# A queue planner with fillers for TensorE and coupled durations, and the softmax quotient moved from GpSimd to VectorE

## The chip, the cores and the metric

The kernel runs on one core of one Trainium2 chip. The metric is the device time in microseconds of one execution, lower is better. Three runs of the kernel before took 5684.96, 5691.24 and 5709.57 us; their median is 5691.24 us.

## The reference

Input is a batch of 32 images, 56 x 56 pixels, 96 channels, all float32. Four layers follow each other:

```python
# layer 0, conditional: four experts, mixed per image
rw = sigmoid(mean(x, (1, 2)) @ Wr + br)
h = relu(bn1(x @ (rw mixes Wpw) + rw @ bpw))          # 96 -> 384
h = relu(bn2(depthwise3x3(h, rw mixes Wdw) + ...))    # 384 channels, nine taps
x = bn3(h @ (rw mixes Wpwl) + rw @ bpwl) + x          # 384 -> 96
# layer 1: x + depthwise5x5(x, fixed kernel)
# layer 2: relu, depthwise3x3, 96 x 96 product, batch norm
# layer 3: shifted-window attention, 7 x 7 windows, 3 heads of 32, then an MLP
s = softmax(q @ k.T / sqrt(32) + mask)
x = x + (s @ v) @ wo + bo                             # q, k, v from layernorm(x)
x = x + gelu(layernorm(x) @ w1 + b1) @ w2 + b2        # 96 -> 384 -> 96
```

## The kernel before

**Tiling and stages.** Each image goes through four stages, written as Python generators.

`stage_router` (line 664) loads the image as `xT` (96 x 3136), sums it on ScalarE, computes the four expert weights and mixes the weights `wmix` and `wmix2` on VectorE.

`stage_conditional` (723) works on twelve blocks, four strips of 14 image rows by three groups of 128 channels. `expand` (728) fills a padded block `h1` by TensorE and ScalarE; then come nine taps into `h2`: the first by ScalarE, the other eight by VectorE `scalar_tensor_tensor` on 128 x 784 elements, the group `h<-h,mix,h` of the profile, 96 per image. `project` (757) brings seven rows back to 96 channels, ScalarE scales them into `y`, and GpSimd adds them to `xT`.

`stage_depthwise` (831) lays four image rows and eight channels on the partitions by DMA and does both fixed convolutions with banded 32 x 32 matmuls on sixteen sub-arrays of TensorE, the group `cv<-x,band`. Its product with `pw` leaves eight row blocks `res`, each of seven image rows in four packs of 98 tokens.

`stage_swin` (979) does, for each of the eight blocks, layernorm (`normalized`, 929, with the power -0.5 on GpSimd), transposes, `wq`, `wk`, `wv`, scores, exponentials on ScalarE, and `kept` (1061), the mask as a product on GpSimd. `averaged` (1076) forms the denominators `pd` (96 x 392, by a matmul with ones) and the unnormalised averages `po` in two PSUM banks. `divided` (1109) makes the quotient, `attended` (1167) multiplies by `wo` and adds to `res` on VectorE (`res<-mm,res`). `hidden` (1178) and `perceptron` (1198) are the MLP; its sum is `tb<-mm,tb`, which goes out by DMA.

**The quotient.** The reciprocal of `pd` is ScalarE's exp(-ln(pd)), improved by one Newton step, out = (-po) r (pd r - 2). ScalarE takes ln and exp, copies `pd` to `den` and `-po` to `num` in SBUF, both with the pixels reordered from windows to rows. GpSimd multiplies `den` by r and `num` by r (the group `hid<-hid,hid`), and VectorE does the last `scalar_tensor_tensor`, `oT<-hid,hid`. The division of block i - 2 is recorded in round i of the loop (line 1311), the averages of block i - 1 after it (1319).

**What sets the order.** Nothing is issued while the stages run. `Recorder.call` (286) notes each instruction with its engine, its buffers, a planned duration from `cost` and `COST` (144) and a target. `interleave` (1352) runs the stages of four images beside each other and sets the target to image number + start + length x progress, by `PLAN` (155). `order` (333) is a list scheduler: each engine that is free takes the instruction with the lowest target whose producers are done, `CROSSING` (156) or `TO_TENSOR` (157) ns earlier, and whose buffers are free. The result is the fixed order of each engine's queue. `give` (421) issues it, so nearly every record in the profile has line 427 and is told apart by its tiles. Rings of buffers limit the run ahead: five PSUM banks `mm` and three `cv` (448), five `hid` (455), two `oT` (465).

A test on the weights selects a general version of layer 3 at run time; with these inputs it doesn't run.

Of the kernel before, what the change touches and what calls it, by code (L numbers as in the profile page):

```python
# [105 lines left out]
def tile_scores_in_range(ctx: ExitStack, tc: tile.TileContext, a: dict, flag: bass.AP):  # L106
# [35 lines left out]


COST = {
    ("vector", "scalar_tensor_tensor"): (180, 1.28), ("vector", "tensor_tensor"): (180, 0.96),
    ("vector", "tensor_scalar"): (190, 0.78), ("vector", "tensor_reduce"): (180, 0.95),
    ("vector", "tensor_copy"): (180, 1.1), ("vector", "reciprocal"): (180, 6.2),
    ("scalar", "activation"): (200, 0.72), ("scalar", "copy"): (200, 0.72),
    ("gpsimd", "tensor_tensor"): (350, 2.4), ("gpsimd", "memset"): (150, 0),
    ("sync", "dma_start"): (550, 0),  # L150
}
LANDING = 3000
IMAGE_LANDING = 12000

PLAN = {"router": (0, 1), "conditional": (0.7, 1), "depthwise": (1.8, 1), "swin": (3.6, 1)}
CROSSING = 350
TO_TENSOR = 700


def cost(engine, method, args, kw):  # L160
    if method == "preload_act_table_set":
        return 1300
    out = kw["out"] if "out" in kw else args[0]
    n = math.prod(out.shape[1:])
    if engine == "tensor":
        if method == "transpose":
            return 127
        k, m = args[1].shape[0], math.prod(args[1].shape[1:])
        if k == 32 and m == 32:
            return 68 * n / 392  # L170
        if k == 32:
            return 86
        if m == 32:
            return 75 if n < 128 else 255
        return 195 if n < 128 else 80 + 1.6 * n
    if len(args) > 3 and args[3] == ALU.pow:
        return 300 + 280 * n
    fixed, each = COST[engine, method]
    if engine == "scalar":
        if kw.get("accum_out") is not None:  # L180
            fixed += 190
        if hasattr(kw.get("scale"), "shape"):
            each += 0.37
        elif hasattr(kw.get("bias"), "shape"):
            each += 0.25
    return fixed + each * n
# [69 lines left out]
class Recorder:  # L256
# [4 lines left out]
    def __init__(self, nc):  # L261
        self.nc = nc
        self.work = []
        self.target = 0.0
        self.open = None
        for engine in self.ENGINES:
            setattr(self, engine, self.Engine(self, engine))

# [64 lines left out]
    def order(self):  # L333

        for n, w in enumerate(self.work):
            w.n = n
            w.waits = len(w.before)
            w.ready = 0.0
            for v in w.before:
                v.after.append(w)  # L340

            w.needs = list(w.starts)
            w.left = None
        for w in self.work:
            for b in w.starts:
                if b.ring.banks:
                    for u in b.users:
                        w.needs.extend(c for c in u.writes if c not in w.needs)
        for w in self.work:
            for b in w.uses:  # L350
                b.left = len(b.users)
        queues = {e: [] for e in self.ENGINES}
        free = dict.fromkeys(self.ENGINES, 0.0)
        events = []
        result = []

        def put(w):
            heapq.heappush(queues[w.engine], (w.target, w.n))

        def available(w):  # L360
            need = {}
            for b in w.needs:
                if b.slot is None:
                    need.setdefault(b.ring, []).append(b.number)
            return all(
                len(n) <= len(ring.free) and (ring.banks or max(n) < ring.begun + len(n)) for ring, n in need.items()
            )

        for w in self.work:
            if not w.waits:  # L370
                put(w)
        now = 0.0
        count = 0
        while len(result) < len(self.work):
            for e in self.ENGINES:
                if free[e] > now:
                    continue
                held = []
                while queues[e]:
                    item = heapq.heappop(queues[e])  # L380
                    w = self.work[item[1]]
                    if not available(w):
                        held.append(item)
                        continue
                    for b in w.needs:
                        if b.slot is None:
                            b.ring.free.sort()
                            b.slot = b.ring.free.pop(0)[1]
                            b.ring.begun += 1
                    result.append(w)  # L390
                    w.start = now
                    free[e] = now + w.ns
                    heapq.heappush(events, (free[e], count, None))
                    heapq.heappush(events, (free[e] + w.landing, count + 1, w))
                    count += 2
                    break
                for item in held:
                    heapq.heappush(queues[e], item)
            assert events, "no work can start"
            now = events[0][0]  # L400
            while events and events[0][0] <= now:
                _, _, w = heapq.heappop(events)
                if w is None:
                    continue
                if isinstance(w, tuple):
                    put(w[0])
                    continue
                for b in w.uses:
                    b.left -= 1
                    if not b.left:  # L410
                        b.ring.free.append((now, b.slot))
                for v in w.after:
                    v.waits -= 1
                    lag = 0 if v.engine == w.engine else TO_TENSOR if v.engine == "tensor" else CROSSING
                    v.ready = max(v.ready, now + lag)
                    if not v.waits:
                        heapq.heappush(events, (v.ready, count, (v,)))
                        count += 1
        return result

    def give(self, tc):
# [9 lines left out]
def kernel(  # L431
# [187 lines left out]
    nc.sync.dma_start(out=wo[:C, :C], in_=a["L3_conv_wo"])  # L619
    nc.sync.dma_start(out=wo[C:, :C], in_=a["L3_conv_bo"].rearrange("(o c) -> o c", o=1))  # L620
    centre_outputs(wo)
    w1 = load([C, M], a["L3_conv_w1"], "w1")
    w2 = load([P, NB, C], a["L3_conv_w2"].rearrange("(k p) f -> p k f", p=P), "w2")
    b2 = wide("L3_conv_b2", True)
# [354 lines left out]
    def stage_swin(b, res):  # L979
# [96 lines left out]
        def averaged(i):  # L1076

            v = rows_of.pop(i)[2]
            e = exps_of.pop(i).part(*every)
            pd = chip.new(mm)  # L1080
            with chip.together():
                for h in range(NH):
                    chip.tensor.matmul(
                        pd[h * HD : (h + 1) * HD, :RT],
                        ones32[:PS],
                        e[:PS, h].rearrange("k j q -> k (j q)"),
                        start=True,
                        stop=True,
                    )
            po = chip.new(mm)  # L1090
            with chip.together():
                for j in range(NP):
                    for h in range(NH):
                        hs = slice(h * HD, (h + 1) * HD)
                        chip.tensor.matmul(
                            po[hs, j * PK : (j + 1) * PK], v[:PS, j, hs], e[:PS, h, j], start=True, stop=True
                        )

            inv, den, num = (chip.new(hids)[:C] for _ in range(3))
            sums, log = by_windows(pd[:C, :RT]), windows_by_rows(inv)  # L1100
            chip.scalar.activation(log, sums, AF.Ln, reads=(tables,))
            chip.scalar.activation(inv, inv, AF.Exp, scale=-1.0, reads=(tables,))
            chip.scalar.copy(windows_by_rows(den), sums)
            chip.scalar.activation(windows_by_rows(num), by_windows(po[:C, :RT]), AF.Copy, scale=-1.0)
            chip.gpsimd.tensor_tensor(den, den, inv, ALU.mult)
            chip.gpsimd.tensor_tensor(num, num, inv, ALU.mult)
            averages[i] = den, num

        def divided(i):
            den, num = averages.pop(i)  # L1110
            oT = turned_out[i] = chip.new(oTs)
            chip.vector.scalar_tensor_tensor(oT[:C], den, 2.0, num, ALU.subtract, ALU.mult)

        def scores(i):

# [184 lines left out]
        for i in range(NROW + 2) if not general else ():  # L1300
# [6 lines left out]
                yield 2  # L1307
            if here:
                kept(i)
            if i > 1:  # L1310
                divided(i - 2)
            if i + 3 < NROW:
                norm1(i + 3)
                yield 1
# [2 lines left out]
                yield 1  # L1317
            if 0 < i <= NROW:
                averaged(i - 1)
                yield 2.5  # L1320
            if i > 1:
                attended(i - 2)
                yield 1.5
# [41 lines left out]
    def when(stage, b):  # L1365

        start, length = PLAN[stage]
        return b + start, length


    residuals = {}
    for step in range(B + 3):
# [59 lines left out]
```

## Time and profile before

| what | value |
|---|---|
| median of 3 runs | 5691.24 us |
| profiled execution, its own time | 5690.76 us |
| its span, first to last instruction | 5689.0 us |
| mean granted TensorE clock | 0.932 |
| TensorE busy, 58442 matmul records | 5303.7 us |
| VectorE busy, 5047 instructions | 4671.9 us |
| ScalarE busy, 8033 instructions | 4098.9 us |
| GpSimd busy, 2942 instructions | 3344.3 us |
| DMA | 166.35 MB, mean 29 GB/s |

PE is TensorE's matmuls, PEld its weight loads, DVE VectorE, ACT ScalarE, POOL GpSimd, SPq the queue of SyncE, which issues the DMAs. A group is named by the tile written, an arrow, and the tiles read. A row of a group gives the count, the total busy time in us, the mean ns of one, then the engine's idle time just ahead of it and who ended most of that. One matmul of the code in float32 stands as two records. A wait row reads: who waited, for whom, us in all, how often, the longest. The clock is a share of full speed.

### The profile page before, as it was taken

The page shows a single profiled execution, that of the slowest core. Times are in us where ns is not written, and L with a number is a line of the kernel's source. Part 1 is how long each engine was busy: PE and PEld are TensorE (multiplying, and loading weights), DVE is VectorE, ACT ScalarE, POOL GpSimd, SP SyncE. Part 2 cuts the span into 40 slices and gives each one's busy share as a digit, 9 for nine tenths or more (in the row PEclk, how much of TensorE's full clock was granted, in tenths as well). Part 3 has the DMA queues.
Part 4 walks back from the last instruction along what each step waited for, and adds up shares of the span by engine and source line. Part 5 has one row for each costly group of instructions (what it writes and reads, how often), then busy time and mean ns, then how long its engine had stood idle before and what let it go on. Part 6 is the DMA issues. An engine that isn't in the chain of part 4 may idle for free.

```text
span 5689.0 us, 139721 instructions
## 1 busy us (share of the span) xinstructions
PE 5303.7 (93%) x58442; PEld 3191.4 (56%) x58442; DVE 4671.9 (82%) x5047; ACT 4098.9 (72%) x8033; POOL 3344.3 (59%) x2942
## 2 busy tenths in 40 slices
PE   3579999999999999999999999999999999999998
PEld 1245555555555555555555556555555555556566
DVE  7998788888888888888888888888889888888621
ACT  3457777777777777777777776777777777777766
POOL 2126665666665666655666665666555666665665
PEclk8789899999999999999999998999999999999999
DMA  1020111111111111111111111101111101111100
GB/s 39 20 41 20 28 32 35 32 26 24 30 33 35 31 24 25 31 32 35 31 24 25 30 33 34 33 20 28 32 33 34 33 20 28 31 33 25 25 19 23
DMA packets 482066, 166.35 MB, mean 29 GB/s; under 512 B 477439, under 2 KB 478100, under 8 KB 478356
## 3 DMA queue, kind: packets, MB, share of 16 engines
q1 hardware_dynamic: 481428, 157.32, 13.0%
q8 instruction: 464, 7.60, 0.6%
q14 instruction: 174, 1.43, 0.1%
HBM read 41.60 MB, written 38.54 MB: 14 GB/s over the span
## 4 chain that ended last, share of the span: by engine, by line
PE 39%; DVE 39%; ACT 9%; POOL 8%; issue 5%; DMA 0%; SPq 0%; DVEq 0%; POOLq 0%; ACTq 0%
DVE h L427 34%; PE mm L427 33%; PE cv L427 7%; ACT h L427 4%; POOL exps L427 4%; ACT hid L427 2%; DVE oT L427 1%; POOL hid L427 1%; DVE res L427 1%; DVE tb L427 1%; DVE var L427 1%; ACT xT L427 1%; ACT lnsq L427 1%; POOL var L427 1%; POOL xT L427 1%
## 5 line engine op out<-in xcount | busy, mean ns | idle before, releaser
L427 DVE SCALAR_TENSOR_TENSOR h<-h,mix,h 128x784 f32<-128x784 f32 x3072 | 3815.4, 1245 | 255.2 <-ACT h L427 176.9
L427 POOL TENSOR_TENSOR hid<-hid,hid 96x392 f32<-96x392 f32 x512 | 744.6, 1470 | 333.1 <-ACT hid L427 327.1
L427 PE MATMUL cv<-x,band 32*32 32x392 f32 x24576 | 916.0, 509 | 5.9 <-ACT x L427 3.7
L427 POOL TENSOR_TENSOR var<-var,mhalf 98x4 f32<-98x4 f32 x512 | 613.5, 1202 | 357.7 <-DVE var L427 181.8
L427 PE MATMUL mm<-xT,wmix 96*128 96x448 f32 (+1 forms) x1536 | 692.4, 553 | 15.7 <-ACT h L427 12.6
L427 PE MATMUL mm<-h,wmix 128*96 128x392 f32 x1536 | 608.3, 538 | 97.4 <-ACT h L427 97.4
L427 POOL TENSOR_TENSOR lnd<-res,var 98x384 f32<-98x384 f32 x512 | 518.6, 1013 | 301.3 <-PE mm L427 262.6
L427 ACT ACTIVATE hid<-mm,c 128x392 f32<-128x392 f32 x768 | 442.0, 583 | 346.4 <-PE mm L427 335.9
L427 PE MATMUL mm<-hT,w 96*128 96x392 f32 x1536 | 626.1, 511 | 27.1 <-DVE tb L427 27.1
L427 ACT ACTIVATE h<-h,biasd,s 128x784 f32<-128x784 f32 x384 | 397.5, 1035 | 350.4 <-DVE h L427 350.3
L427 POOL TENSOR_TENSOR xT<-y,xT 96x392 f32<-96x392 f32 x256 | 342.4, 1338 | 506.0 <-ACT y L427 466.1
L427 PEld LDWEIGHTS mm<-w,hid 128*98 128x98 f32 x6144 | 561.7, 167 | 57.6 <-issue 30.6
L427 ACT ACTIVATE h<-mm,bias,s 128x448 f32<-128x448 f32 (+1 forms) x768 | 538.8, 709 | 63.6 <-PE mm L427 56.7
L427 PE MATMUL mm<-w,hid 128*98 128x96 f32 x6144 | 577.3, 250 | 0.4 <-ACT hid L427 0.4
L427 ACT ACTIVATE exps<-mm 49x196 f32<-49x196 f32 x1536 | 507.1, 330 | 88.7 <-PE mm L427 64.9
L427 POOL TENSOR_TENSOR tb<-res 98x384 f32<-98x384 f32 x256 | 318.3, 1243 | 369.3 <-DMA out<-tb 193.3
L427 PEld LDWEIGHTS cv<-x,band 32*32 32x32 f32 x24576 | 331.4, 103 | 362.4 <-issue 260.0
L427 DVE TENSOR_REDUCE var<-lnsq 98x4 f32<-98x388 f32 x512 | 266.5, 547 | 263.6 <-ACT lnsq L427 174.0
L427 PEld LDWEIGHTS mm<-h,wmix 128*96 128x96 f32 x1536 | 260.8, 178 | 384.4 <-issue 220.3
L427 PEld LDWEIGHTS mm<-hT,w 96*128 96x128 f32 x1536 | 260.6, 190 | 270.3 <-issue 102.1
L427 ACT ACTIVATE hid<-mm 96x392 f32<-96x392 f32 x512 | 253.2, 495 | 204.9 <-PE mm L427 198.9
L427 POOL TENSOR_TENSOR tb<-tb,L_conv_b 98x384 f32<-98x384 f32 x256 | 390.2, 1524 | 12.6
(127 smaller groups left out, 7722.1 us busy)
## 6 DMA issues: line engine op xcount, KB each, us to landing
xT<-in_x SPq DMA_DIRECT2D x32, 1176.0 KB
x<-xT SPq DMA_DIRECT2D x384, 98.0 KB
out<-tb SPq DMA_DIRECT2D x256, 147.0 KB
filtered<-x SPq DMA_DIRECT2D x384, 49.0 KB
filtered<-x SPq DMA_DIRECT2D x384, 42.0 KB
filtered<-x SPq DMA_DIRECT2D x384, 7.0 KB
wpw<-in_L_conv_Wpw SPq DMA_DIRECT2D x1, 576.0 KB
wpwl<-in_L_conv_Wpwl SPq DMA_DIRECT2D x4, 144.0 KB
```

Source lines behind the costliest of these rows:

```text
L427: getattr(getattr(self.nc, w.engine), method)(*args, **kw)
```

## The change

The planner gets new prices, stage targets and a lag to TensorE that depends on the producer. While a GpSimd instruction and a VectorE `scalar_tensor_tensor` run beside each other, each is planned `SHARING` times slower. When TensorE has had nothing to do for `SPARE_AFTER` ns and a bank of `mm` is free, the planner puts in a filler, a 128 x 128 matmul of the identity with itself, whose result nobody reads.

In the quotient, ScalarE's two copies and GpSimd's two products go. VectorE reads `pd` and `po` from their banks: step = pd r, step = (step - 2) r, and oT = step x po with the pixels reordered. `wo` is negated once for the sign. The division is recorded right after the averages of the same block.

```diff
 COST = {
-    ("vector", "scalar_tensor_tensor"): (180, 1.28), ("vector", "tensor_tensor"): (180, 0.96),
+    ("vector", "scalar_tensor_tensor"): (150, 1.16), ("vector", "tensor_tensor"): (180, 0.96),
...
-    ("gpsimd", "tensor_tensor"): (350, 2.4), ("gpsimd", "memset"): (150, 0),
+    ("gpsimd", "tensor_tensor"): (200, 2.1), ("gpsimd", "memset"): (150, 0),
...
-PLAN = {"router": (0, 1), "conditional": (0.7, 1), "depthwise": (1.8, 1), "swin": (3.6, 1)}
+PLAN = {"router": (0, 1), "conditional": (0.56, 0.85), "depthwise": (1.6, 0.47), "swin": (3.35, 1)}
 CROSSING = 350
-TO_TENSOR = 700
+
+TO_TENSOR = {"vector": 1500, "gpsimd": 1500, "scalar": 1000, "sync": 700}
+SPARE_AFTER = 250
+SHARING = 1.36
...
     if len(args) > 3 and args[3] == ALU.pow:
-        return 300 + 280 * n
+        return 200 + 200 * n
...
-            each += 0.37
+            each += 0.37 if hasattr(kw.get("bias"), "shape") else 0.23
...
+        def share(now):
+
+            nonlocal count
+            rate = SHARING if len(running) > 1 else 1.0
+            for r in running.values():
+                r["left"] -= (now - r["since"]) / r["rate"]
+                r["since"], r["rate"] = now, rate
+                r["end"] = free[r["work"].engine] = now + max(r["left"], 0.0) * rate
+                heapq.heappush(events, (r["end"], count, r))
+                count += 1
...
+            if e == "gpsimd" or w.calls[0][0] == "scalar_tensor_tensor":
+                running[e] = {"work": w, "left": w.ns, "since": now, "rate": 1.0}
+                share(now)
+                return
...
+                else:
+                    if e == "tensor" and self.spare and now >= free[e] + SPARE_AFTER and self.spare[2].free:
+                        lhs, rhs, ring = self.spare
+                        w = Work(e, 0.0)
+                        b = Buffer(ring)
+                        operands = View(b, ring.tiles[0])[:, : rhs.shape[1]], lhs, rhs
+                        w.calls.append(("matmul", operands, {"start": True, "stop": True}))
+                        w.ns = cost(e, "matmul", operands, {})
+                        w.needs, w.starts, w.uses, w.writes = [b], [b], [b], [b]
+                        b.users[w], b.left, b.owner = True, 1, w
...
+                        begin(w)
...
     centre_outputs(wo)
+    if not general:
+        nc.vector.tensor_scalar(wo[:C], wo[:C], -1.0, None, ALU.mult)
...
-            inv, den, num = (chip.new(hids)[:C] for _ in range(3))
-            sums, log = by_windows(pd[:C, :RT]), windows_by_rows(inv)
-            chip.scalar.activation(log, sums, AF.Ln, reads=(tables,))
+            inv = chip.new(hids)[:C]
+            chip.scalar.activation(inv, pd[:C, :RT], AF.Ln, reads=(tables,))
             chip.scalar.activation(inv, inv, AF.Exp, scale=-1.0, reads=(tables,))
-            chip.scalar.copy(windows_by_rows(den), sums)
-            chip.scalar.activation(windows_by_rows(num), by_windows(po[:C, :RT]), AF.Copy, scale=-1.0)
-            chip.gpsimd.tensor_tensor(den, den, inv, ALU.mult)
-            chip.gpsimd.tensor_tensor(num, num, inv, ALU.mult)
-            averages[i] = den, num
+            averages[i] = pd, po, inv
 
         def divided(i):
-            den, num = averages.pop(i)
+
+            pd, po, inv = averages.pop(i)
+            step = chip.new(hids)[:C]
+            chip.vector.tensor_tensor(step, pd[:C, :RT], inv, ALU.mult)
+            chip.vector.scalar_tensor_tensor(step, step, 2.0, inv, ALU.subtract, ALU.mult)
             oT = turned_out[i] = chip.new(oTs)
-            chip.vector.scalar_tensor_tensor(oT[:C], den, 2.0, num, ALU.subtract, ALU.mult)
+            chip.vector.tensor_tensor(
+                oT[:C].rearrange("c (r n w) -> c r n w", n=NWIN, w=7),
+                by_windows(step),
+                by_windows(po[:C, :RT]),
+                ALU.mult,
+            )
...
-            if i > 1:
-                divided(i - 2)
...
                 averaged(i - 1)
-                yield 2.5
+                yield 1.5
+                divided(i - 1)
+                yield 1
...
+    chip.spare = ident, ident, mm
```

More of the change, by code (lines that the diff above doesn't have):

```diff
@@ L265, in __init__ @@
         self.open = None
+        self.spare = None
         for engine in self.ENGINES:
@@ L367, in available, with done @@
             )
+        running = {}
+        def share(now):
[7 more added lines that the diff above has]
+                count += 1
+        def done(w, now):
+            for b in w.uses:
+                b.left -= 1
+                if not b.left:
+                    b.ring.free.append((now, b.slot))
+            for v in w.after:
+                v.waits -= 1
+                lag = 0 if v.engine == w.engine else TO_TENSOR[w.engine] if v.engine == "tensor" else CROSSING
+                v.ready = max(v.ready, now + lag)
+                if not v.waits:
+                    ready.append(v)
         for w in self.work:
@@ L373, in order, with begin @@
         count = 0
-        while len(result) < len(self.work):
+        def begin(w):
+            nonlocal count
+            for b in w.needs:
+                if b.slot is None:
+                    b.ring.free.sort()
+                    b.slot = b.ring.free.pop(0)[1]
+                    b.ring.begun += 1
+            result.append(w)
+            w.start = now
+            e = w.engine
+            if e == "gpsimd" or w.calls[0][0] == "scalar_tensor_tensor":
+                running[e] = {"work": w, "left": w.ns, "since": now, "rate": 1.0}
+                share(now)
+                return
+            free[e] = now + w.ns
+            heapq.heappush(events, (free[e], count, None))
+            heapq.heappush(events, (free[e] + w.landing, count + 1, w))
+            count += 2
+            if e == "tensor":
+                heapq.heappush(events, (free[e] + SPARE_AFTER, count, None))
+                count += 1
+        left = len(self.work)
+        spares = 0
+        while left:
             for e in self.ENGINES:
@@ L384, in order @@
                         continue
[L385 to L395, printed above, removed]
-                    break
+                    begin(w)
+                    left -= 1
+                    if e == "tensor":
+                        spares = 0
+                    break
+                else:
[8 more added lines that the diff above has]
+                        b.users[w], b.left, b.owner = True, 1, w
+                        spares += 1
+                        assert spares < 10000, "no work can start"
+                        begin(w)
                 for item in held:
@@ L400, in order @@
             now = events[0][0]
+            ready = []
             while events and events[0][0] <= now:
                 _, _, w = heapq.heappop(events)
-                if w is None:
-                    continue
                 if isinstance(w, tuple):
                     put(w[0])
[L407 to L418, printed above, removed]
+                elif isinstance(w, dict):
+                    if w["end"] == now and running.get(w["work"].engine) is w:
+                        del running[w["work"].engine]
+                        w["work"].end = now
+                        done(w["work"], now)
+                        share(now)
+                elif w is not None:
+                    done(w, now)
+            for v in ready:
+                heapq.heappush(events, (v.ready, count, (v,)))
+                count += 1
         return result
```

## The prediction

> **What bounds the kernel now.** I read the shares of the page first, then its slices, the busy time by stretches, the waits, and last the groups by tile.
>
> ```profile
> PE 5303.7 (93%) x58442; PEld 3191.4 (56%) x58442; DVE 4671.9 (82%) x5047; ACT 4098.9 (72%) x8033; POOL 3344.3 (59%) x2942
> ...
> DVE  7998788888888888888888888888889888888621
> ...
> PEclk8789899999999999999999998999999999999999
> ```
>
> TensorE and VectorE are both nearly full, and the granted clock sits at 0.9, not 1. The last slices have an almost idle VectorE. The 32 loads of an image start at 29 us, 423 us (the fifth) and 5048 us (the last), so I cut the span there and where VectorE falls off:
>
> ```profile
> 423.00:5048.00 4625.00, 4463.37 (x49296) 2669.34 (x49296) 3971.33 (x4212) 3453.30 (x6777) 2861.96 (x2457) 0.94 0.14 30
> 5048.00:5304.00 256.00, 248.35 (x2919) 147.43 (x2918) 216.42 (x227) 188.59 (x377) 160.13 (x134) 0.92 0.11 23
> 5304.00:5689.00 385.00, 362.79 (x4258) 257.90 (x4256) 123.56 (x168) 266.93 (x588) 229.46 (x254) 0.99 0.11 24
> 0.00:423.00 423.00, 229.23 (x1974) 116.71 (x1974) 360.58 (x443) 190.06 (x294) 92.70 (x97) 0.78 0.15 32
> ```
>
> Columns after the length are busy us of PE, PEld, DVE, ACT, POOL, then clock and DMA. The first row is 27 equal periods of 171.3 us. VectorE works 3971/27 = 147 us of each; it is idle for 12.2% of 1000 to 5000 us (gaps above 150 ns), 20.9 us a period. TensorE is idle only 3.4%, 5.9 us, but part of its busy time is stretched. One period, cut where the granted clock changes:
>
> ```profile
> 2479.70:2493.40 13.70, 13.25 (x95) 8.40 (x95) 10.90 (x11) 10.47 (x25) 5.37 (x5) 0.50 0.31 79
> 2493.40:2503.60 10.20, 8.28 (x93) 5.62 (x91) 9.67 (x9) 6.75 (x13) 6.55 (x7) 1.00 0.00 0
> 2503.60:2510.40 6.80, 6.80 (x13) 2.63 (x13) 6.66 (x7) 4.30 (x11) 4.19 (x3) 0.50 0.00 0
> 2510.40:2650.30 139.90, 135.84 (x1623) 80.75 (x1623) 118.16 (x130) 105.02 (x203) 88.21 (x78) 1.00 0.13 28
> ```
>
> For 20.5 us TensorE runs at half clock though it is busy: matmul pairs that take 0.66 us elsewhere take 1.3. The timeline has an idle TensorE ahead of each dip, 2.49 us and 1.40 us long, both before wo<-oT, both waiting for VectorE's oT. At full clock that work would take about 10 us less. So TensorE needs some 171 - 6 - 10 = 155 us a period and VectorE 150 with its short issue gaps: neither binds alone, the order of the queues couples them.
>
> ```profile
> DVE h L427 <- ACT h L427: 135.3, 70, 2.8
> DVE res L427 <- PE mm L427: 120.9, 54, 4.9
> DVE var L427 <- ACT lnsq L427: 115.3, 23, 5.8
> DVE wmix L427 <- ACT wmix L427: 48.1, 23, 2.1
> ```
>
> These are VectorE's waits from 1000 to 5000 us: head-of-queue waits, spread over many producers, which is what a plan with wrong durations leaves. The groups concerned:
>
> ```profile
> L427 DVE SCALAR_TENSOR_TENSOR h<-h,mix,h 128x784 f32<-128x784 f32 x3072 | 3815.4, 1245 | 255.2 <-ACT h L427 176.9
> L427 POOL TENSOR_TENSOR hid<-hid,hid 96x392 f32<-96x392 f32 x512 | 744.6, 1470 | 333.1 <-ACT hid L427 327.1
> L427 DVE SCALAR_TENSOR_TENSOR oT<-hid,hid 96x392 f32<-96x392 f32 x256 | 190.1, 743 | 83.2 <-POOL hid L427 83.2
> L427 DVE TENSOR_TENSOR res<-mm,res 98x388 f32<-98x388 f32 x256 | 142.1, 555 | 234.7 <-PE mm L427 208.8 <-ACT hid L427 21.2 <-ACT slots L427 4.4
> ```
>
> (The last row stands so in the groups by form.)
>
> [...] record by record, the 1109 h taps with no POOL tensor work beside them average 1032 ns and the 750 wholly beside it 1408; a line through all is 1012 ns plus 0.34 ns per ns of overlap. res<-mm,res, one input in PSUM, never leaves 544 to 565 ns. [...] The trace has only 0.5 and 1.0, but its dips follow gaps of 1.4 and 2.5 us, and recovery takes 7 to 14 us.
>
> **The change, part by part**, against the profiled execution: span 5689.0, 1.8 outside it, 5690.8; the median of the runs is 5691.2, so nothing is corrected.
>
> (1) POOL loses 512 hid<-hid,hid. They lie beside h taps for 533 us; 533 x 0.34 = 181 us off VectorE, 5.7 a period. If other POOL work slides into the freed place, only 3.
>
> (2) VectorE gains two TENSOR_TENSOR per row with a PSUM input, 512 in all. Price from res<-mm,res: 0.47 us start to start where the next instruction is independent, 0.59 where it isn't. I take 0.53: 16 x 0.53 = 8.5 us a period. The third, the old oT multiply, stays and comes from 743 ns towards its median of 556, for 8 rows about -1.1. Net with (1): +1.7 us a period, between -0.5 and +7. The single negation of wo is ahead of everything, 0.3 us.
>
> (3) ScalarE loses 512 copies out of PSUM, 8 x 2 x 0.48 = 7.7 us a period; at 72% that is worth nothing by itself. The way from averages to wo loses a copy (0.47) and POOL's two multiplies (1.47 each) and gains one PSUM multiply: about 2 us shorter, at the place where TensorE's long gaps begin (its waits for oT: 68.7 us in 4000, 2.9 a period). The new first multiply waits for ScalarE's Exp; behind it in VectorE's queue stand the h taps, and behind those ScalarE's ReLUs and TensorE's projections. The built order puts single taps between the three steps in most rows, so a late Exp costs a part of a tap. pd and po are now held until VectorE has read them, 1 to 4 us longer, 16 of about 161 bank uses a period: some 35 bank-us of 5 x 171.
>
> (4) Fillers: the built order has 643 matmuls of ident by ident, 375 of them ahead of the fourth image's router, 91 after the last projection, but only 3 or 4 per period from the tenth image on. By the 96-column pairs (2 x 87 ns) one costs about 0.25 us: 1 us a period at most, nothing where TensorE waits. Gain: the two dips, up to 10 us; fillers stand where the plan has gaps, not where the chip has them, so I take half with (3): 5. Bound from below: 0.
>
> (5) The plan's prices now match what I measure uncontended: tap 150 + 1.16 x 784 = 1059 (1032), POOL multiply 200 + 2.1 x 392 = 1023 (86 such records alone: 1021), pow 1000 (1053), and the coupling 1.36 is 1408/1032. The planned lag to TensorE rises from 700 to 1500. The stage targets start swin a quarter of an image sooner; the built order still leaves the same 24 attention rows after the last projection as before, so I count nothing for that. What remains of VectorE's 20.9 us idle is a choice: I take 11.5, a bit over half, since lags, ScalarE's and the banks' waits stay. Period: 150 + 1.7 + 11.5 = 163.2. From TensorE's side: 155 + 1 filler + 2 idle + 5 of the dips = 163. Bounds: 157, where both engines run almost closed up, and 170, if only the dips shrink.
>
> DMAs keep their count (1879 on SP's queue, by the order) and its share is low (DMA 0.14); SP is passed by nothing that binds.
>
> (6) Ends. Until 423 us VectorE is busy 361 of it; the fill is the first images' taps, and warm matmuls save little: 420. From 5304 TensorE works through three images of attention and MLP alone, 106 us each; shorter rows and 8 us less ScalarE give perhaps 4%: 370.
>
> Sum: 420 + 27 x 163.2 (4406) + 1.5 x 163.2 (245) + 370 + 1.8 = 5443, rounded to **5445 us**.
>
> **Rivals.** *Nearly closed* (0.19): the plan holds on the chip. 420 + 28.5 x 157 + 365 + 2 = 5262; with spread 5230 to 5360. For it: so few fillers per period mean a plan with hardly a gap. Against: 12% idle today under the same planner. *Dips only* (0.15): durations were not the cause, the waits move; 28.5 x 168.5 + 792 = 5594, spread 5560 to 5660. *No change* (0.04): the shorter rows just pay for (2); 5690. *PSUM banks, slower* (0.12): pd and po wait in VectorE's queue behind taps of 1.0 to 1.4 us; TensorE's order is fixed, so a missing bank stops it. If each row stops it 1.5 us more, 12 us a period, against 8 gained: +4 x 28.5 = 5800. It decides from 1 us a row on. For it: 161 uses share 5 banks, 5.3 us each; against: 35 bank-us is 4%, and the plan counts banks.
>
> **The numbers.** Forecast 0.50, own range 5370 to 5540. Range 8 in 10: 5250 to 5660; outside lie the lowest of the closed case, no change and the slower case. Faster by over 0.5% (about what a measurement of this kernel tells from no change): 0.84; within: 0.04; slower: 0.12.
>
> **What would show it.** (1) h taps mean 1245 to about 1190; (2) two new groups near 555 ns; VectorE busy in total near 4720, share of the span 86 to 88%; (3) TensorE's waits for oT below 40 us in all; (4) clock above 0.95; (5) period near 163 us between loads, VectorE idle under 9% there. It is wrong if the period stays over 168, or if the waits of TensorE for VectorE's or ScalarE's reads of mm grow by 1 us a row.

## The result, and the profile after

The changed kernel takes **5517.49 us**, the median of four runs (5507.19 to 5532.91), beside 5688.1 us for the kernel before on the same chip: ratio **0.9701 [0.9675, 0.9727]**, 3.0% faster. Below, *before* and *after* name the two kernels. The profiled execution took 5517.6 us, of which its span is 5515.8.

The busy shares and slices of the page of the kernel after:

```profile
PE 5272.6 (96%) x59728; PEld 3163.2 (57%) x59728; DVE 4448.2 (81%) x5560; ACT 3881.5 (70%) x7521; POOL 3310.2 (60%) x2430
...
DVE  6997768888888897888898788888878888887622
...
PEclk8999999999999999999999999999999999999999
```

TensorE went from 93% to 96% of a shorter span; 643 fillers are 1286 of its records. VectorE has 513 instructions more and is busy 224 us less; the prediction had it busier. POOL lost 512 instructions and is busy only 34 us less, so the others take longer on average.

The stretches of the kernel after, cut at the same events as before (loads of the fifth and the last image, then where VectorE falls off). Columns after the length are busy us of PE, PEld, DVE, ACT, POOL, then clock and DMA:

```profile
0.00:410.00 410.00, 314.78 (x2840) 205.14 (x2841) 338.53 (x459) 195.09 (x305) 195.50 (x96) 0.91 0.15 33
410.00:4881.00 4471.00, 4340.88 (x49618) 2556.64 (x49619) 3761.28 (x4635) 3265.39 (x6344) 2771.79 (x2029) 0.98 0.14 31
4881.00:5130.00 249.00, 241.97 (x2917) 136.59 (x2912) 207.80 (x255) 175.42 (x342) 153.99 (x102) 0.95 0.11 24
5130.00:5516.00 386.00, 374.93 (x4360) 264.78 (x4359) 140.59 (x215) 245.59 (x533) 188.90 (x206) 1.00 0.10 23
```

The 27 periods take 4471 us, 165.6 each, where they took 171.3. The first three, read between loads, are 172, 184 and 178 us; the other 24 average 164.0. TensorE is busy for 97% of this stretch. Idle time in gaps above 150 ns, counted from the trace between 1000 and 4800 us, is 2.3% for TensorE (3.5% before) and 14.2% for VectorE (12.2% before). The chain of work that ended last agrees: TensorE carries 64% of it and VectorE 17%, each 39% before. By busy time and by this chain TensorE now binds.

The waits of VectorE in the kernel after, 1000 to 5000 us (who, for whom, us in all, times, longest):

```profile
DVE hid L486 <- ACT hid L486: 113.7, 75, 5.0
DVE h L486 <- ACT h L486: 83.8, 80, 4.4
DVE res L486 <- PE mm L486: 81.0, 67, 2.8
DVE var L486 <- POOL lnd L486: 72.9, 48, 7.0
```

The largest is the new one, the first multiply of the quotient waiting for ScalarE's Exp. TensorE's waits in the same stretch:

```profile
PE mm L486 <- POOL exps L486: 31.7, 23, 2.6
...
PE mm L486 <- DVE hid L486: 9.8, 15, 1.6
```

Its waits for oT, which stood ahead of the clock dips before, are not in the list any more. Before, in the same stretch:

```profile
PE mm L427 <- DVE oT L427: 68.7, 45, 2.5
```

The groups of the kernel after, by form (`lnd<-res,var` is GpSimd's scaling in the layernorm, `tb<-res` its first step of the MLP's sum):

```profile
L486 DVE SCALAR_TENSOR_TENSOR h<-h,mix,h 128x784 f32<-128x784 f32 x3072 | 3398.4, 1143 | 138.8 <-ACT h L486 128.0
L486 DVE SCALAR_TENSOR_TENSOR hid<-hid,hid 96x392 f32<-96x392 f32 x256 | 184.3, 720 | 1.6
L486 DVE TENSOR_TENSOR hid<-mm,hid 96x392 f32<-96x392 f32 x256 | 142.6, 557 | 245.9 <-ACT hid L486 214.1 <-PE cv L486 21.2 <-PE mm L486 10.2
L486 DVE TENSOR_TENSOR oT<-hid,mm 96x392 f32<-96x392 f32 x256 | 140.9, 551 | 12.5 <-PE mm L486 8.0
L486 POOL TENSOR_TENSOR lnd<-res,var 98x384 f32<-98x384 f32 x512 | 737.5, 1444 | 324.1 <-PE mm L486 297.9
```

The h tap takes 1143 ns instead of 1245. And 3072 taps of 1143 ns are 3511 us, more than the 3398.4 us that the group is busy: taps now overlap. Before, 3072 x 1245 = 3825 against 3815.4: hardly any overlap. The planner of after lets the taps of two blocks alternate, so that a tap doesn't need the one just ahead of it. This comes from a detail of the diff that the excerpt above leaves out, and two experiments below take it alone: in the old `order`, a tap's successor enters the queue at the very event that ends the tap, so the next choice can take the same block again; the new one collects such work in `ready` and queues it when VectorE has already chosen another. Where a tap follows a tap within 150 ns, the median step from start to start is 946 ns in after and 1071 ns before (means 1103 and 1269). In exchange POOL's lnd went from 1013 ns to 1444.

### The profile page after: what moved, and what is told of

Same layout as the page of the kernel before. It is cut to its first block, busy times and chain, and to the rows that moved or that the text cites. A ratio compares the mean times of both kernels' runs of the same rounds, so it can differ in the third digit from the quotient of the medians.

```text
span 5515.8 us, 141640 instructions
## 1 busy us (share of the span) xinstructions
PE 5272.6 (96%) x59728; PEld 3163.2 (57%) x59728; DVE 4448.2 (81%) x5560; ACT 3881.5 (70%) x7521; POOL 3310.2 (60%) x2430
## 3 DMA queue, kind: packets, MB, share of 16 engines
q1 hardware_dynamic: 481428, 157.32, 13.3%
## 4 chain that ended last, share of the span: by engine, by line
PE 64%; DVE 17%; ACT 8%; POOL 7%; issue 3%; DMA 0%; SPq 0%; ACTq 0%; POOLq 0%; DVEq 0%
PE mm L486 51%; PE cv L486 13%; DVE h L486 13%; POOL tb L486 4%; ACT h L486 3%; ACT exps L486 1%; POOL xT L486 1%; DVE hid L486 1%; DVE tb L486 1%; POOL exps L486 1%; ACT hid L486 1%; DVE wmix L486 1%; ACT slots L486 1%; DVE var L486 0%; POOL lnd L486 0%
## 5 line engine op out<-in xcount | busy, mean ns | idle before, releaser
L486 DVE SCALAR_TENSOR_TENSOR h<-h,mix,h 128x784 f32<-128x784 f32 x3072 | 3398.4, 1143 | 138.8 <-ACT h L486 128.0
L486 POOL TENSOR_TENSOR var<-var,mhalf 98x4 f32<-98x4 f32 x512 | 797.7, 1562 | 600.6 <-DVE var L486 574.8
L486 PE MATMUL cv<-x,band 32*32 32x392 f32 x24576 | 962.1, 511 | 0.0
L486 POOL TENSOR_TENSOR lnd<-res,var 98x384 f32<-98x384 f32 x512 | 737.5, 1444 | 324.1 <-PE mm L486 297.9
L486 POOL TENSOR_TENSOR xT<-y,xT 96x392 f32<-96x392 f32 x256 | 496.7, 1942 | 442.2 <-ACT y L486 420.2
L486 POOL TENSOR_TENSOR tb<-res 98x384 f32<-98x384 f32 x256 | 529.8, 2070 | 308.0 <-DVE res L486 152.0
L486 PE MATMUL mm<-h,wmix 128*96 128x392 f32 x1536 | 566.1, 509 | 9.1 <-ACT h L486 9.0
L486 PEld LDWEIGHTS cv<-x,band 32*32 32x32 f32 x24576 | 226.9, 103 | 358.2 <-issue 283.1
L486 PEld LDWEIGHTS mm<-xT,wmix 96*128 96x128 f32 x1536 | 264.3, 196 | 232.2 <-issue 104.4
L486 ACT ACTIVATE h<-h,mix 128x784 f32<-128x784 f32 x384 | 364.2, 949 | 11.0 <-POOL h L486 5.4
```

What stands on the lines that cost most here:

```text
L486: getattr(getattr(self.nc, w.engine), method)(*args, **kw)
```

## Experiments

The theory at first was the prediction's: prices that match the chip close the gaps of the plan. The rival: the quotient alone does most of it. After the first results came a third: which taps stand beside each other (the alternation). Every ratio is against the kernel before, run on the same chip.

**The quotient alone**: the kernel before with the new quotient, its place in the loop and the negated `wo`; planner and prices are the old ones.

```diff
-            chip.scalar.copy(windows_by_rows(den), sums)
-            chip.scalar.activation(windows_by_rows(num), by_windows(po[:C, :RT]), AF.Copy, scale=-1.0)
-            chip.gpsimd.tensor_tensor(den, den, inv, ALU.mult)
-            chip.gpsimd.tensor_tensor(num, num, inv, ALU.mult)
-            averages[i] = den, num
+            averages[i] = pd, po, inv
...
+            chip.vector.tensor_tensor(step, pd[:C, :RT], inv, ALU.mult)
+            chip.vector.scalar_tensor_tensor(step, step, 2.0, inv, ALU.subtract, ALU.mult)
```

> The old planner with the new quotient. Theory (planner and quotient both carry the gain; the quotient is the smaller part, by 2 us less way per row and 5.7 us a period less contention): 5640 us, the h taps fall from 1245 to about 1190 ns. Rival (the quotient alone is just more VectorE work in a plan that doesn't fit): 5690 to 5750 us, TensorE's waits for VectorE grow.

Measured 5532.65 us, 0.9743 [0.9711, 0.9775]: nearly the whole gain, and more than either expectation. Its tap group, then VectorE's waits in this kernel, 1000 to 5000 us, and TensorE's for oT:

```profile
L427 DVE SCALAR_TENSOR_TENSOR h<-h,mix,h 128x784 f32<-128x784 f32 x3072 | 3614.2, 1180 | 251.1 <-ACT h L427 172.7
```

```profile
DVE h L427 <- ACT h L427: 137.3, 73, 2.6
DVE hid L427 <- ACT hid L427: 100.5, 32, 3.8
...
DVE res L427 <- PE mm L427: 2.0, 3, 0.9
```

```profile
PE mm L427 <- DVE oT L427: 6.0, 15, 0.4
```

res<-mm fell from 120.9 us to 2.0, and var's wait for ScalarE's lnsq, 115.3 before, is gone from the list; TensorE's waits for oT fell from 68.7 to 6.0. The wait for Exp is new, 100.5. VectorE's idle share fell from 12.2% to 8.1%, and the period to 165.1 us.

**The place alone**: in the kernel before, only the division is recorded right after its averages; the POOL products stay.

```diff
-            if i > 1:
-                divided(i - 2)
...
-                yield 2.5
+                yield 1.5
+                divided(i - 1)
+                yield 1
```

> The kernel before with only the place of the division changed: recorded right after the averages of its block, still with ScalarE's copies and GpSimd's products. Theory (the quotient's gain, 5533 us, comes from taking work off GpSimd[...]): 5690 us within 30, as GpSimd's two products still stand in the way. Rival (it comes from the earlier place in the plan): 5600 us or less.

Measured 5702.09 us, 1.0019 [1.0009, 1.0028]. The place by itself gives nothing; the gain needs the new operations. Whether they would do as well at the old place was not run. The taps are at 1222 ns here, against 1245 before, so up to 23 of the 65 ns by which the quotient alone shortens them can come without taking anything off POOL.

**The planner alone**: the kernel after with the old quotient at its old place, `wo` not negated.

```diff
-            inv = chip.new(hids)[:C]
+            inv, den, num = (chip.new(hids)[:C] for _ in range(3))
...
+            chip.gpsimd.tensor_tensor(den, den, inv, ALU.mult)
+            chip.gpsimd.tensor_tensor(num, num, inv, ALU.mult)
```

> The new planner with the old quotient (copies on ScalarE, products on GpSimd). Theory (the planner carries most of the gain): 5560 us, clock above 0.96. Rival (the gain needs the shorter path from averages to wo): above 5630 us, and TensorE's waits for oT stay near 90 us.

Measured 5602.7 us, 0.9854 [0.9833, 0.9876]. VectorE's largest wait in this kernel:

```profile
DVE oT L486 <- POOL hid L486: 251.9, 110, 5.3
```

POOL still has the products here, and with alternating taps its other groups take longer (var 1970 ns against 1202 before, tb<-res 2080 against 1243); so it stands on the way to oT. The time lies between the two expectations. The two parts alone gain 155 us (5688 - 5533) and 85 us (5688 - 5603), 240 together, and the whole 170: the gains overlap by 70 us.

**No fillers**: the kernel after without them.

```diff
-    chip.spare = ident, ident, mm
```

> The changed kernel without the 643 fillers. Theory (the fillers keep the clock up in the fill, the order does it in the periods): clock 0.95, 5550 us, the loss within the first 410 us. Rival 1 (the fillers in the periods prevent the dips): 5600 us or more, dips of 14 us back in each period. Rival 2 (they do nothing): 5517 us within 10.

Measured 5520.41 us, 0.9711 [0.9679, 0.9743]: 3 us from after, inside the intervals, as the second rival had it. The second, third and fifth slice of its clock fall back:

```profile
PEclk8789899999999999999999999999999999999999
```

By stretches the clock is 0.87 instead of 0.94 in the first 1000 us, and 0.98 in both kernels from 1000 to 4800. The fillers raise the clock at the start of the run without shortening it: up to the load of the fifth image 410 us with them and 413 without, the next three periods 534 and 536. From 1000 to 4800 us the clock is 0.98, too, in the quotient alone, which has no fillers, and in the planner alone, which has the old quotient: the dips of the middle go with either part.

**Chained taps**: the kernel after, with ready work queued at once, as in the old planner, so that the taps of a block follow each other; prices, coupling, targets and fillers stay.

```diff
-            for v in ready:
-                heapq.heappush(events, (v.ready, count, (v,)))
-                count += 1
+                for v in ready:
+                    heapq.heappush(events, (v.ready, count, (v,)))
+                    count += 1
+                ready.clear()
```

> The changed kernel, but work that becomes ready at a moment is queued before the engines choose at that moment, as in the old planner, so the taps of one block follow each other again instead of alternating with other VectorE work. Theory (alternating is what makes taps cheap: no wait for the tap before[...]): taps back from 1143 to about 1240 ns, about 0.12 us more from tap to tap, VectorE busy 4750 us, time 5600 us. Rival (TensorE now binds, so VectorE's tap time is hidden): taps slower too, but the time within 25 us of 5517.

Measured 5692.71 us, 1.0010 [1.0001, 1.0020]: with every new price, the coupling, the fillers and the quotient, the gain is gone, and more than the theory's 5600. The taps are chained again (median step 1071 ns), yet a tap takes only 1166 ns, not the 1240 expected, and VectorE's busy time is 4707.4 us, 259 more than in after:

```profile
L487 DVE SCALAR_TENSOR_TENSOR h<-h,mix,h 128x784 f32<-128x784 f32 x3072 | 3566.7, 1166 | 213.3 <-ACT h L487 135.8
```

The largest wait of TensorE in this kernel, and then that of VectorE:

```profile
PE mm L487 <- DVE tb L487: 144.6, 107, 3.0
```

```profile
DVE var L487 <- POOL lnd L487: 225.3, 77, 9.4
```

POOL works faster here (lnd 954 ns), yet VectorE waits for it more: over the whole span POOL stands idle 487 us ahead of lnd for TensorE's product, and TensorE in turn waits for VectorE's tb. (The idle time ahead of lnd doesn't tell this kernel from a fast one: it is 503 us in the quotient alone.) The granted clock is 0.976, above that of after. The loss stands in the plan already: from the eighth image's load on, the planner puts 27 fillers into a period where after has 4, so it expected TensorE to find nothing to do.

**Chained taps without fillers**: both edits.

> The changed kernel with chained taps (5693 us with fillers) and without fillers. Theory (there the 1177 fillers stand in TensorE's fixed queue and wait for banks, 134 us of idle before them in 3800, which then holds up real matmuls): 5600 us. Rival 1 (fillers only take time that TensorE had to spare, as in the changed kernel, where leaving them out gave 5520 for 5517): 5693 within 20. Rival 2 (without them the clock falls and it gets slower): 5730.

Measured 5680.02 us, 0.9990 [0.9980, 0.9999]: as the first rival had it, fillers are not what holds the chained version up. TensorE's idle time goes from 9.4 us a period to 14.9 and its busy time from 162.4 to 156.5: the fillers had filled gaps. (The quotient alone is idle 7.1, after 4.8.) The wait moves to another place:

```profile
PE mm L487 <- ACT h L487: 276.9, 47, 9.6
```

**Alternation in the kernel before**, with nothing else changed:

```diff
+            ready = []
...
-                        heapq.heappush(events, (v.ready, count, (v,)))
-                        count += 1
+                        ready.append(v)
+            for v in ready:
+                heapq.heappush(events, (v.ready, count, (v,)))
+                count += 1
```

> The kernel before with one thing changed: work that becomes ready at a moment is queued after the engines have chosen at that moment, so taps alternate with other VectorE work. Theory (alternating makes taps cheaper on the chip, in any plan): taps about 1150 ns instead of 1245, VectorE busy 300 us less, time 5600 us. Rival (alternating only repairs what the new prices spoil): 5690 us within 25, taps cheaper or not.

Measured 5974.39 us, 1.0509 [1.0492, 1.0527]. Taps fell to 1147 ns as in after and VectorE's busy time by 380 us to 4292.3, but its idle share went from 12.2% to 24.6%:

```profile
DVE res L430 <- PE mm L430: 482.6, 108, 7.7
```

Neither expectation came: cheaper taps and a slower kernel. POOL pays here: tb<-res takes 2655 ns instead of 1243 in the mean, and its median hardly moves (1434 and 1383); what grows is the longest, from 1562 ns to 11489. The last section shows where such records come from.

**Alternation with the quotient**: the same edit on the quotient alone.

> The old planner with the new quotient (5533 us) and with alternating taps. Theory (both gains are independent): 5440 us, under the changed kernel, taps about 1120 ns. Rival 1 (alternating only repairs what the new prices spoil): 5533 within 25. Rival 2 (alternating slows GpSimd, and GpSimd's layernorm steps then bind): over 5560 us.

Measured 5663.24 us, 0.9962 [0.9943, 0.9981]. With the products off POOL alternation costs less, but under the old planner it still costs 131 us beside 5532.65. As the second rival had it, VectorE waits for the layernorm on POOL: 183.2 us for lnd, 21.0 in the quotient alone.

**No coupling**: the kernel after with `SHARING` at 1.

```diff
-SHARING = 1.36
+SHARING = 1.0
```

> The changed kernel with the planned coupling of GpSimd and taps set from 1.36 to 1.0, so both are planned at their time alone. Theory (with alternating taps the chip slows GpSimd alone, so the coupling misplans the taps): 5490 us. Rival (the planned slow-down keeps consumers of GpSimd late enough): 5580 us, TensorE's waits for GpSimd and VectorE grow.

Measured 5690.93 us, 1.0008 [0.9999, 1.0017]. A plan that doesn't count the slowdown expects POOL too early:

```profile
DVE var L486 <- POOL lnd L486: 254.4, 73, 10.4
```

It was 72.9 us in after. In this plan alternation without the coupling gains nothing. Chained taps without the coupling were not run.

**Old stage targets** in the kernel after:

```diff
-PLAN = {"router": (0, 1), "conditional": (0.56, 0.85), "depthwise": (1.6, 0.47), "swin": (3.35, 1)}
+PLAN = {"router": (0, 1), "conditional": (0.7, 1), "depthwise": (1.8, 1), "swin": (3.6, 1)}
```

> The changed kernel with the stage targets of the kernel before. Theory (the targets are a minor part): 5517 us within 30. Rival (they belong to the new prices and carry much of the planner's part): 5600 us or more, the periods longer than 168 us.

Measured 5614.56 us, 0.9882 [0.9860, 0.9904]: 97 us lost, as the rival had it.

**A small nudge**: the kernel after with 30 ns more planned for a crossing between engines, to see what any change of the order moves.

```diff
-CROSSING = 350
+CROSSING = 380
```

> The changed kernel with one planner number moved a little: the lag between engines from 350 to 380 ns, nothing else. Theory (how well a fixed order fits the chip is partly luck, so small planner changes move the time by as much as the planner's whole share over the quotient alone, 15 us): some 30 to 100 us either way. Rival (the time follows the planner's prices smoothly): 5517 within 15.

Measured 5582.19 us, 0.9813 [0.9786, 0.9839]: 65 us lost. The wait of TensorE that grew most is that for the mask's product on POOL, 31.7 us in after:

```profile
PE mm L486 <- POOL exps L486: 84.5, 24, 5.0
```

**Taps and products by themselves**: a small kernel that leaves the whole computation of the reference out and runs streams of 96 taps and 96 POOL products of the kernel's shapes, alone and beside each other; taps chained on one accumulator or alternating between two.

```diff
+                acc = accs[n % chains]
+                v.scalar_tensor_tensor(acc, view, tap, acc, ALU.mult, ALU.add)
...
+                g.tensor_tensor(prods[n % 4], a, b, ALU.mult)
```

> A small kernel that leaves the whole computation out: streams of 96 taps (128 x 784) on VectorE, in one chain or alternating between two accumulators, alone and beside a stream of 96 GpSimd products (96 x 392), and GpSimd alone. Theory (a chained tap leaves a pause[...], alternating taps leave none): alone 1030 ns each, from start to start 1070 chained and 950 alternating; beside GpSimd the chained taps rise to about 1400 with GpSimd at about 1500, the alternating ones stay near 1030 to 1150 and GpSimd goes to 2000 or more. Rival (who pays doesn't depend on the chaining): both kinds of taps near 1400 and GpSimd the same beside both.

The program took 628.1 us, one run. Its groups by form:

```profile
L45 POOL TENSOR_TENSOR sharealterg<-a,b 96x392 f32<-96x392 f32 x96 | 163.8, 1745 | 0.1
L45 POOL TENSOR_TENSOR sharechaing<-a,b 96x392 f32<-96x392 f32 x96 | 163.5, 1741 | 0.1
L43 DVE SCALAR_TENSOR_TENSOR sharealterh<-image,tap,sharealterh 128x784 f32<-128x784 f32 x96 | 163.0, 1774 | 0.0
L43 DVE SCALAR_TENSOR_TENSOR sharechainh<-image,tap,sharechainh 128x784 f32<-128x784 f32 x96 | 159.5, 1661 | 3.4
L43 DVE SCALAR_TENSOR_TENSOR alonechainh<-image,tap,alonechainh 128x784 f32<-128x784 f32 x96 | 100.0, 1042 | 3.5
L45 POOL TENSOR_TENSOR poolaloneg<-a,b 96x392 f32<-96x392 f32 x96 | 92.8, 1005 | 0.1
L43 DVE SCALAR_TENSOR_TENSOR alonealterh<-image,tap,alonealterh 128x784 f32<-128x784 f32 x96 | 91.7, 1029 | 0.0
```

Alone, alternating taps start every 954 ns and chained ones every 1077. Beside POOL both kinds take one and the same step, 1.70 us for a tap and a product together. Chaining thus doesn't decide who pays where both streams are dense, as the rival had it, though at 1661 to 1774 ns a tap instead of 1400.

## Why the prediction was right, and where it was wrong

By stretches, predicted and measured: fill 420 and 410; 27 periods 4406 and 4471; the next one and a half 245 and 249; end 370 and 386; outside 1.8 in both. The sum was 5443 and the profiled execution took 5517.6, inside both ranges. Of the 65 us by which the periods are longer than predicted, 45 are in the first three (534 against 3 x 163.2 = 490). The direction and 70% of the size (173 of 246 us) were right; the reason given for the larger part of it was not.

**(1) Taps, right in size.** Predicted 5.7 us a period from the products that leave POOL. The quotient alone, which keeps the old planner, has 1180 ns against 1245: 96 x 65 = 6.2 us. That all of it comes from POOL is not shown, since the place alone has 1222 with the products still there.

**(2) VectorE's price, right.** The new groups are 557 and 551 ns. Busy time was predicted near 4720; the quotient alone has 4719.1. A period of it has 165.1 - 13.3 idle = 151.8 us of work, where the sum said 150 + 1.7 = 151.7. After itself has only 165.6 x 0.858 = 142: the alternation, which no step of the prediction has (with chained taps it is 171.7 x 0.883 = 151.6). The `scalar_tensor_tensor` of the quotient was taken to fall from 743 to its median of 556; it is 616 with the quotient alone and 720 in after, 8 x 0.16 = 1.3 us a period more than taken.

**(3) The shorter way to oT, right, and worth more than I gave it.** TensorE's waits for oT went from 68.7 us to 6.0 in the quotient alone, and the clock from 1000 to 4800 us from 0.94 to 0.98. The idle time of VectorE fell with them, from 20.9 to 13.3 us a period. Counted at VectorE, that is the whole gain of the quotient in a period: work +1.4, idle -7.6, together -6.2 us. Late oT, half clock, late mm and a waiting res<-mm read as one loop that the shorter row opens; the runs show its parts fall together, not which of them would do alone. The cost named for it came too: VectorE waits 100 to 114 us of 4000 for Exp.

**(4) Fillers, wrong in size and place.** Half of the two dips was given to them and (3) together; without fillers the time is 3 us higher, within the intervals, and the middle clock the same. What the fillers raised is the clock of the first 1000 us, from 0.87 to 0.94. The time didn't follow: up to the load of the fifth image 410 us with them and 413 without.

**(5) The failed step.** It read: "The plan's prices now match what I measure uncontended", and from there VectorE's idle falls from 20.9 to 11.5 us a period. In after it rose to 165.6 x 0.142 = 23.5. The sum of the step came out nearly right (163.2 against 165.6) because two errors of opposite sign met: 12 us more idle, and some 9.6 us less work from alternating taps (151.7 against 142). An idle time near 11.5 did appear, 13.3, but in the quotient alone with every old price; and with every new price and chained taps the gain was gone (5692.71). No run has the new prices by themselves. What I missed in the diff is where ready work is queued. VectorE also stopped being the measure: TensorE, fillers included, is busy 160.8 us of 165.6, so closing VectorE's gaps has little left to gain.

**What the planner is worth.** On top of the quotient it brings 5532.65 - 5517.49 = 15 us, and the two intervals meet (0.9711 and 0.9727). By stretches of the two profiled executions that small difference hides two larger ones: the first three periods take 534 us in after and 490 in the quotient alone, 44 lost, and the fill, the other 24 periods and the end together are 50 us shorter (24 x 164.0 against 24 x 165.3 is most of it). The slow start is there without fillers too (536) and was not traced further. Yet taking out a single piece of the planner costs more than the 15 us: coupling 173, alternation 175, targets 97; and moving one number, the crossing, by 30 ns costs 65. So these are numbers set for each other, and the costs of taking one out do not add up to what they bring; how much of each is the piece, and how much any changed order, one nudge can't say. Why the plan with chained taps has gaps under the new prices stays open; whether the planned coupling makes them, no run tells.

**The rivals.** The closed plan (157 us a period) did not come: the last fifteen periods of after are 163.4. "Dips only" had the right mechanism, dips gone and other waits in their place, but too long a period: 168.5 us against 165.1 in the quotient alone. The banks decide from 1 us a row; TensorE waits for VectorE's first reads 9.8 us in 4000, 0.05 us for each of the 193 block rows of that time (4000 / 165.6 x 8).

## What to carry to other kernels

Take the parts of such a change apart before crediting the one with the most lines: here taking two small products off GpSimd and two copies off ScalarE, for two more multiplies on VectorE, gave 0.9743, and the planner added no difference that these intervals separate. In a diff of a list scheduler, read when work becomes ready as closely as its prices, since a tie decides which of two chains goes next. Look at the longest record of a group as well as at its mean: alternation shortened VectorE's taps (946 ns from start to start instead of 1071, in the median) and left single GpSimd records of up to 12 us in the middle of the run. Read such a plan as a tuned point: a nudge of 30 ns moved the time by 1.2%, so a piece taken out shows that the rest was set with it, not what it is worth.

## What the runs showed of the hardware

**Taps beside GpSimd.** The dense streams give the price: 1.70 us for a tap and a product together, where they take 1.08 (0.95 alternating) and 0.97 alone, so a pair saves 0.2 to 0.35 us of what its two instructions would take one after the other. The products there take 1.74 us in the mean beside either kind of tap. The kernel is less even. VectorE and then POOL in one stretch of the kernel after, by the timeline (start, length, instruction):

```profile
2493.83 5.76 DVE L486 SCALAR_TENSOR_TENSOR h<-h,mix,h 128x784 f32<-128x784 f32 x6
...
2511.17 11.82 DVE L486 SCALAR_TENSOR_TENSOR h<-h,mix,h 128x784 f32<-128x784 f32 x8
```

```profile
2494.79 6.27 POOL L486 TENSOR_TENSOR lnd<-res,var 98x384 f32<-98x384 f32 x2 [2.75 <-PE mm L486]
...
2514.59 1.71 POOL L486 TENSOR_TENSOR tb<-tb,L_conv_b 98x384 f32<-98x384 f32 x1
```

The six taps from 2493.83 run at 0.96 us each, as if alone, while POOL needs 6.27 us for two lnd; the eight from 2511.17 take 1.48 each beside TENSOR_TENSOR records of POOL of 1.49 to 1.75 us. The first kind goes further. Here one tb<-res, 0.82 us at its shortest, lasts as long as a train of twelve taps:

```profile
2606.80 11.43 DVE L486 SCALAR_TENSOR_TENSOR h<-h,mix,h 128x784 f32<-128x784 f32 x12
```

```profile
2606.95 11.96 POOL L486 TENSOR_TENSOR tb<-res 98x384 f32<-98x384 f32 x1 [5.65 <-DVE res L486]
```

It starts 0.15 us into the train and ends 0.68 us after it. This goes with alternation. From 100 us on, 137 POOL records of after last over 2.5 us, and 89 to 178 in each other kernel with alternating taps, where the taps beside them start every 946 ns; before, the quotient alone, the place alone and both kernels with chained taps have one such record together. So in these kernels GpSimd's records beside chained trains stay within 2.5 us but for that one, and beside an alternating train one can last to the train's end, as this one of 11.96 us does. Why GpSimd takes that long beside one alternating train and 1.7 us beside another, as in the dense streams, is not settled by these runs.

**Dependent and independent instructions of VectorE.** A tap that reads what the tap just ahead of it wrote costs 1077 - 954 = 123 ns more from start to start, in streams with nothing beside them. The medians in the kernels agree: 1071 ns before and 946 in after.

**Clock and time.** Records at half clock add up to 774 us before, 324 after, 396 with the quotient alone, 277 with chained taps (which take 5693 us) and 482 without fillers (5520 us). The granted clock of the whole does not order these kernels by time.
